# A weight fold spread over idle slots: its last part given slots of its own, and a buffer of its own

## The chip, the cores and the metric

The kernel runs on one core of one Trainium2 chip. The metric is the time of one execution on the device, in microseconds (us). Below, PE is the matmul engine (TensorE), PEld its weight loads, DVE the vector engine, ACT the scalar engine, POOL GpSimd and SP the engine whose queue issues most transfers.

## What is computed

One decoder layer on a batch of 16 sequences of 512 tokens and 256 features, all in float32: causal attention with 16 heads, LoRA terms on q and v and rotary positions, a residual and a layer norm, then a feed-forward part, a residual and a layer norm. The feed-forward part is the one that matters here:

```python
h = jnp.einsum('bsd,dh->bsh', x, W_exp) + b_exp
h = butterfly(h, up_weights, D_HIDDEN)
h = jax.nn.gelu(h + up_bias, approximate=False)
h = butterfly(h, down_weights, D_HIDDEN)
y = jnp.einsum('bsh,hd->bsd', h, W_con) + b_con
return y + down_bias
```

D_HIDDEN is 1024. A butterfly is ten linear stages; stage s mixes each pair of hidden units whose numbers differ in bit s. It is linear, so the kernel multiplies it into the weights once (the **fold**): the up side into W_exp, the down side into W_con. After that each sequence needs two plain matrix products, an expansion (256 to 1024) and a contraction (1024 to 256).

## The kernel before

**Slots.** All work is written out in one order by hand. The loop `for s in range(-head, last)` (line 827) runs over slots; five slots make one quad (half of the heads of one 128-feature chunk, even or odd), 20 slots one sequence b. In a slot, PE computes score blocks twice: `largest` (lines 411 to 442) for the row maxima, which DVE reduces (L430, "the reduces"), and `weights` (462 to 509), 15 slots behind, whose blocks ACT exponentiates (L493) and POOL masks (L497). The two kinds alternate in two PSUM tiles, pb and pa, with one buffer each: the pb and pa matmuls of a slot wait until exp and the reduces of the slot before have read them. Then come, in this order, `weigh` (probabilities times v, tile po, L521), the other tasks of the slot (`others[s]`), its `holes`, and last the fold tasks due in it (lines 870 to 876). Each engine runs its own instructions strictly in this order.

**Around slot 45.** For sequence 0, `turn_x1` stands in slot 45 (line 746): PE transposes the normed rows, DVE copies them to x1T (L617), POOL adds a bias over all of z (L621). `hidden` (628 to 646), the expansion product, takes slots 46 to 49, two of eight pieces a slot (tile ph, L633); DVE empties pieces 0 and 4 (L644), ACT the others (L646). Slot 50 has the gelus (ACT) and four projections of a later sequence (PE, tile pqk). `contract` (655 to 669), which reads the folded down weights `wdn`, starts in slot 51. `normalize` of sequence 0 (reciprocal and product on DVE, L553 and L554) is in slots 27, 28, 29, 31 and 36, 37, 39, 40.

**Fold tasks.** Every task is a pair (begin, rest). Begins run up to three tasks ahead of rests (line 872). There are these kinds:

- `across_chunks` (224 to 244): a stage 7, 8 or 9 for one pair of the eight 128-unit chunks. Begin is two ACT instructions into tiles x (tag `cross`, four buffers, L232), rest two DVE instructions (L239). The down side takes stages 9, 8, 7 in this order, four pairs each; the up side takes only stage 9 so.
- `across_by_products` (246 to 274): the same for stages 7 and 8 of the up side. Begin is four ACT instructions (L255), rest eight PE matmuls (L267, tile pd) and two ACT copies (L272).
- `multiply_paths` (205 to 215): six products on DVE (L215) that build, step by step, the matrices of stages 0 to 6 from path factors; the last is 1024 wide.
- `within_chunk` (217 to 222): such a matrix times one chunk; two PE instructions into a PSUM tile `fold` (L219) and an ACT copy (L222).
- `up_done` (291 to 298): four transposes (L294) and a DVE copy (L295) that put the folded up weights into `wup`.

`fold_tasks` (309 to 329) gives two lists. The first, the up side within chunks, is done in slots 3 to 14. The second has 44 tasks: 12 stage pairs, 6 products and 8 chunks of the down side, mixed evenly with 14 tasks of the up side, then four `up_done`. Lines 809 to 811 spread them evenly by count over slots 15 to 44.

**Buffers.** `yb` (line 113) is used twice: first for the path factors of the down side (loaded by `load_factors(1)`, line 127), then as `wup`. All PSUM tiles of the tag "w" (ph, fold, pd, pqk, pwo, py and the transposes) share three buffers.

## Time and profile before

| | us |
|---|---|
| median of three runs | 1359.33 |
| lowest, highest | 1358.64, 1360.84 |
| the profiled execution, its own time | 1357.15 |
| its span in the profile | 1355.4 |
| PE busy | 1320.3 |
| DVE busy | 925.8 |
| ACT busy | 707.3 |
| POOL busy | 510.9 |

The span is what the profile covers; 1.75 us of the execution lie around it. A row of the profile names the line, engine and operation, the tile written and those read, the number of instructions, their busy time and the mean of one in ns, and what ended the idle time ahead of them. A row of busy time by stretch has the stretch, its length, then PE, PEld, DVE, ACT and POOL busy with instruction counts, the clock granted to PE as a share of full speed, the busy share of the transfer engines and GB/s. A row of the timeline has a start, a duration and an instruction; equal neighbours are merged.

### The profile page before, as it was taken

How to read it: one execution, taken by the hardware profiler on the slowest of the kernel's cores; microseconds unless marked ns; L12 is line 12 of the kernel's file. 1: busy time of each engine (PE TensorE's matmuls, PEld its weight loads, DVE VectorE, ACT ScalarE, POOL GpSimd, SP SyncE). 2: the span in 40 equal slices, each digit the busy share in tenths (PEclk: the TensorE clock that was granted, in tenths of full speed). 3: DMA queues.
4: the chain of work that ended last, by engine and by line, in shares of the span. 5: the costliest groups of instructions: out<-in, count | busy, mean ns of one | idle time of the engine just before them, and what ended most of it. 6: DMA issues, size and time to landing. Idle time of an engine off the chain costs nothing.

```text
span 1355.4 us, 23859 instructions
## 1 busy us (share of the span) xinstructions
PE 1320.3 (97%) x8728; PEld 702.5 (52%) x8728; DVE 925.8 (68%) x2949; ACT 707.3 (52%) x1079; POOL 510.9 (38%) x777
## 2 busy tenths in 40 slices
PE   8898999999999999999999999999999999998998
PEld 4453545455454545555454554545555454554555
DVE  4788757667685766758577685857768685776632
ACT  2575454454646445464645545464554546445643
POOL 3534215344251533425153352515335252531311
PEclk9998999999999999999999999999999999999999
DMA  5311010110102011010110101010110101000000
GB/s 172 120 45 45 22 59 30 40 45 30 68 30 74 30 41 45 30 67 30 67 35 31 57 30 68 30 60 30 40 60 30 68 30 55 30 27 32 30 12 31
DMA packets 45685, 63.49 MB, mean 47 GB/s; under 512 B 5752, under 2 KB 26232, under 8 KB 45568
## 3 DMA queue, kind: packets, MB, share of 16 engines
q1 hardware_dynamic: 41680, 56.42, 11.8%
q10 hardware_dynamic: 3888, 5.55, 1.3%
q8 instruction: 69, 1.13, 0.3%
q14 instruction: 48, 0.39, 0.1%
HBM read 23.40 MB, written 8.91 MB: 24 GB/s over the span
## 4 chain that ended last, share of the span: by engine, by line
PE 84%; DVE 11%; ACT 3%; issue 2%; DMA 0%; POOLq 0%; POOL 0%; DVEq 0%; SPq 0%; ACTq 0%
PE pb L479 19%; PE ph L633 17%; PE py L660 16%; PE po L521 10%; PE pqk L337 8%; DVE junk L430 5%; PE pvv L383 4%; PE pwo L559 3%; PE pa L421 3%; DVE bn L577 1%; PE pb L421 1%; PE pt L616 1%; ACT pT L493 1%; PE pa L479 1%; DVE z L567 1%
## 5 line engine op out<-in xcount | busy, mean ns | idle before, releaser
L430 DVE CUSTOM_DVE_ANT_0 junk<-pa,causal 128x384 bf16<-128x384 f32 (+2 forms) x878 | 438.3, 499 | 235.0 <-PE pa L421 176.1
L493 ACT ACTIVATE pT<-pb 128x1024 f32<-128x1024 f32 (+1 forms) x314 | 293.8, 936 | 377.3 <-PE pa L421 227.6
L497 POOL TENSOR_SCALAR_AFFINE_SELECT pT<-pT 128x256 f32<-128x256 f32 x512 | 202.5, 407 | 733.3 <-ACT pT L493 731.6
L479 PE MATMUL pb<-qz,kz 17*128 17x512 f32 (+2 forms) x1756 | 328.8, 473 | 16.1 <-ACT pT L493 12.1
L421 PE MATMUL pa<-kz,qz 32*128 32x384 f32 (+3 forms) x1756 | 329.2, 474 | 4.2 <-DVE mx L430 4.2
L660 PE MATMUL py<-wdn,h 128*128 128x256 f32 x1024 | 252.1, 391 | 0.0
L479 PEld LDWEIGHTS pb<-qz,kz 17*128 17x128 f32 (+1 forms) x1756 | 142.9, 183 | 179.5 <-issue 82.2
L633 PE MATMUL ph<-x1T,yb 128*128 128x512 f32 x512 | 235.8, 604 | 0.0
L660 PEld LDWEIGHTS py<-wdn,h 128*128 128x128 f32 x1024 | 185.1, 189 | 72.2 <-issue 36.2
L521 PE MATMUL po<-pT,vaug 128*32 128x512 f32 (+3 forms) x2048 | 179.5, 446 | 0.0
L633 PEld LDWEIGHTS ph<-x1T,yb 128*128 128x128 f32 x512 | 92.4, 189 | 122.3 <-issue 97.6
L421 PEld LDWEIGHTS pa<-kz,qz 32*128 32x128 f32 (+1 forms) x1756 | 143.7, 184 | 13.6 <-DVE mx L430 11.2
L553 DVE RECIPROCAL sums<-sums 128x128 f32<-128x128 f32 x128 | 121.1, 946 | 0.0
L337 PE MATMUL pqk<-xT,wqk 128*128 128x512 f32 x256 | 118.5, 613 | 0.0
L646 ACT COPY h<-ph 128x512 f32<-128x512 f32 x84 | 49.2, 585 | 123.2 <-PE ph L633 123.2
L521 PEld LDWEIGHTS po<-pT,vaug 128*32 128x32 f32 x2048 | 47.1, 109 | 102.3 <-issue 78.2
L430 DVE DVE_READ_ACCUMULATOR2_ANT mx<- 128x1 f32 x1024 | 84.5, 82 | 0.0
L337 PEld LDWEIGHTS pqk<-xT,wqk 128*128 128x128 f32 x256 | 48.0, 194 | 61.9 <-issue 57.4
L365 POOL TENSOR_TENSOR swap<-swap,rope_sb 128x512 f32<-128x512 f32 x62 | 79.6, 1283 | 0.0
L602 ACT ACTIVATE z<-z,norm 128x256 f32<-128x256 f32 x128 | 66.7, 589 | 24.6 <-DVE norm L595 24.5
L668 DVE TENSOR_TENSOR z<-py,z 128x256 f32<-128x256 f32 x64 | 27.1, 423 | 74.1 <-PE py L660 73.9
L430 DVE CUSTOM_DVE_ANT_0 junk<-pb,causal 128x256 bf16<-128x256 f32 (+3 forms) x146 | 63.6, 436 | 17.3 <-PE pa L421 4.0
(91 smaller groups left out, 1334.2 us busy)
## 6 DMA issues: line engine op xcount, KB each, us to landing
xT<-in_xT SPq DMA_DIRECT2D x16, 512.0 KB
swap<-qz SPq DMA_DIRECT2D x64, 128.0 KB
swap<-kz SPq DMA_DIRECT2D x64, 128.0 KB
z<-in_x SPq DMA_DIRECT2D x16, 512.0 KB
sums<-x SPq DMA_DIRECT2D x64, 128.0 KB
out_y<-z SPq DMA_DIRECT2D x15, 512.0 KB
x<-x SPq DMA_DIRECT2D x32, 128.0 KB
early<-in_wexpT ACTq DMA_DIRECT2D x1, 1028.0 KB
```

Source lines behind the costliest of these rows:

```text
L337: nc.tensor.matmul(pq, wqk[:, d, e : e + P], xTs[b][:, d, :], start=(d == 0), stop=(d == NC - 1))
L365: engine.tensor_tensor(swap, swap, rope_sb[:, 1, :], ALU.mult)
L421: lambda i=i, rows=rows, at=at, n=n, t=t, ps=ps: nc.tensor.matmul(ps[:, i, at : at + n], q[rows, par, t * P : n], k_[rows, par, 0:n], star ...
L430: lambda i=i, at=at, n=n, t=t, g=g, ps=ps: nc.vector.tensor_tensor_reduce(out=junk[:, 0:n], in0=ps[:, i, at : at + n], in1=causal[:, T - n ...
L479: lambda i=i, rows=rows, at=at, n=n, k=block, ps=ps: nc.tensor.matmul(ps[:, i, at : at + n], kt[rows, par, k * P : (k + 1) * P], qt[rows, ...
L493: nc.scalar.activation(pT[:, heads, 0:n], ps[:, :, at : at + n], AF.Exp)
L497: nc.gpsimd.affine_select(out=diag, in_=diag, pattern=[[0, 2], [1, P]], compare_op=ALU.is_ge, fill=0.0, base=0, channel_multiplier=-1,)
L521: nc.tensor.matmul(po[HG * g : HG * (g + 1), k * P : T], vaugs[b % 2][:, k, NG * c + g, first : first + HG], pT[:, g, at : at + n], start= ...
L553: nc.vector.reciprocal(sums[:, ts], sums[:, ts])
L602: nc.scalar.activation(zs[b][:, t, :], zs[b][:, t, :], AF.Identity, bias=norm[:, 2, t : t + 1], scale=norm[:, 1, t : t + 1],)
L633: nc.tensor.matmul(ph, wup[:, c, hc * P : (hc + 1) * P], state["x1T", b][:, c, :], start=(c == 0), stop=(c == NC - 1),)
L660: nc.tensor.matmul(py, state["h", b][:, hc, t * P : (t + 1) * P], wdn[:, hc, :], start=(hc == 0), stop=(hc == NHC - 1),)
```

## The change

The down side's list is cut after its first eight tasks (stages 9 and 8). Those stay mixed with the up side; with `up_done` that is 26 tasks, spread by the same rule over slots 15 to 44. The other 18, in the old order (four pairs of stage 7, six products, eight chunks), form a third list, given by count to slots 45 to 49: four tasks, four, three, four, three. So the rests are the four pairs in slot 45, products 1 to 4 in slot 46, products 5 and 6 and the first chunk in slot 47, four chunks in 48, three in 49. The begins of the first two pairs run in slots 42 and 43. The path factors of the down side get a tile of their own (8128 bytes a partition), since `up_done` now writes `wup`, in `yb`, before they are used.

The tasks that stay are placed anew, too, since 26 and not 44 share the slots. Of the stages of the down side, stage 9 has its rests in slots 16, 19, 21 and 25 (before: 15 to 18), stage 8 in 28, 32, 34 and 38 (before: 19 to 22). Of the up side, the rests by products are in 15, 17, 18, 20, 23, 24, 26 and 27 (before: 15, 17, 19, 21, 23, 25, 27 and 29), those of stage 9 in 30, 31, 33 and 35 (before: 31, 33, 35 and 36), and `up_done` in 40 to 43 (before: 42, 42, 43, 44).

```diff
-    factors[1] = yb[:, 0:nfac]
+    factors[1] = const.tile([P, nfac], F32, name="factors1")
...
-        def down():
-            yield from all_across(1, wdn, D)
-            yield from all_within(1, wdn, D)
-
-
-        last = [
+
+
+        down = list(all_across(1, wdn, D))
+        late = down[2 * NHC // 2 :] + list(all_within(1, wdn, D))
+        up_last = [
             (idle, lambda d=d, half=half: up_done(d, half))
             for d in range(NC)
             for half in range(2)
         ]
-        return list(all_within(0, ya, DA)), mixed(down(), up()) + last
+        return list(all_within(0, ya, DA)), mixed(down[: 2 * NHC // 2], up()) + up_last, late
...
-    first, second = fold_tasks()
-    fold = first + second
+    first, second, third = fold_tasks()
+    fold = first + second + third
     tasks_at = dict(zip(range(2, behind), (0, 1, 2, 3, 4, 4, 5, 5, 5, 6, 9, 11, 14)))
-    for s in range(behind, 2 * per + 5):
-        tasks_at[s] = len(first) + -(-len(second) * (s - behind + 1) // (2 * per + 5 - behind))
+    needed = 2 * per + 5
+    for s in range(behind, needed):
+        tasks_at[s] = len(first) + -(-len(second) * (s - behind + 1) // (needed - behind))
+    for s in range(needed, needed + 5):
+        tasks_at[s] = len(first + second) + -(-len(third) * (s - needed + 1) // 5)
```

## The prediction

> **What bounds the kernel now.** I read the page first, then busy time by stretch, the waits of the matmul engine in the early stretch, and the order of instructions around slot 45.

> ```profile
> span 1355.4 us, 23859 instructions
> ...
> PE 1320.3 (97%) x8728; PEld 702.5 (52%) x8728; DVE 925.8 (68%) x2949; ACT 707.3 (52%) x1079; POOL 510.9 (38%) x777
> ...
> PE   8898999999999999999999999999999999998998
> ...
> DVE  4788757667685766758577685857768685776632
> ACT  2575454454646445464645545464554546445643
> ...
> PEclk9998999999999999999999999999999999999999
> ```

> PE (matmul) bounds nearly all of it; only the first five of 40 slices show idle PE and a lower clock. The whole fold lies there. By stretch (PE, PEld, DVE, ACT, POOL busy, clock):

> ```profile
> 55.43:93.39 37.96, 32.36 (x254) 17.85 (x254) 27.78 (x90) 32.46 (x77) 9.66 (x19) 1.00 0.08 27
> 93.39:121.98 28.59, 24.70 (x179) 11.70 (x178) 26.96 (x76) 15.88 (x31) 14.97 (x22) 1.00 0.18 63
> 121.98:166.21 44.23, 41.22 (x281) 22.12 (x282) 31.94 (x105) 21.50 (x38) 11.27 (x22) 0.85 0.07 23
> 166.21:189.75 23.54, 23.54 (x138) 10.19 (x137) 14.72 (x43) 8.70 (x12) 5.47 (x9) 1.00 0.10 34
> 189.75:198.45 8.70, 8.70 (x34) 3.42 (x33) 3.48 (x7) 8.03 (x12) 0.41 (x1) 1.00 0.20 75
> ```

> Slot starts come from the timeline of PE, where the pb and pa matmuls of each slot stand in order. These rows are slots 15-25 (**A**: ACT 86% busy), 26-33 (**B**: DVE 94%), 34-44 (**C**: PE at clock 0.85), 45-49 (**D**: PE without a gap, DVE 63%, ACT 37%), and 50. In A and B PE stands idle 66.55 - 57.06 = 9.5 us:

> ```profile
> PE pb L479 <- ACT pT L493: 5.7, 7, 1.9
> PE pa L421 <- DVE mx L430: 2.1, 3, 1.1
> ```

> The moved work, before:

> ```profile
> L239 DVE SCALAR_TENSOR_TENSOR wdn<-wdn,coefs,x 128x256 f32<-128x256 f32 x24 | 13.2, 591 | 0.0
> L219 PE MATMUL fold<-wdn,yb 128*128 128x256 f32 x16 | 6.1, 482 | 0.0
> L215 DVE TENSOR_TENSOR yb<-yb 128x32 f32<-128x32 f32 (+5 forms) x6 | 4.1, 690 | 0.1
> ```

> [...] L239 takes 0.478 at the median but 1.492 at most, as in the pair (two instructions, 1.90) that meets a POOL add:

> ```profile
> 130.76 1.90 DVE L239 SCALAR_TENSOR_TENSOR early<-early,coefs,x 128x257 f32<-128x257 f32 x2
> ```
> ```profile
> 130.87 1.49 POOL L367 TENSOR_TENSOR kz<-kz,swap 128x512 f32<-128x512 f32 x1
> ```

> [...] Here a window with 1.75 us of PE is followed by two at half:

> ```profile
> 118.40:121.80 3.40, 1.75 (x16) 0.91 (x16) 3.26 (x9) 1.02 (x1) 1.40 (x3) 0.99 0.04 11
> 121.80:125.20 3.40, 3.22 (x20) 1.61 (x24) 2.20 (x9) 0.76 (x2) 0.97 (x2) 0.50 0.00 0
> 125.20:128.60 3.40, 3.40 (x20) 1.89 (x16) 0.81 (x4) 2.58 (x6) 1.68 (x3) 0.51 0.00 0
> ```

> **The change, part by part.** All is set against the profiled execution (1357.15, of which 1355.4 span). The median of the runs is 1359.33, 2.18 above it; I add the difference to that median. No instruction is added or dropped: the lists are redistributed.

> *A, slots 15-25.* The list now holds 26 tasks for 30 slots, not 44, so tasks run thinner, and of the twelve stage tasks of the down side only four fall in A. By the lists, ACT loses eight pairs of L232 there (2 x 0.503 each, 8.0) and gets one more group of four L255 of the up side (1.3): -6.7 us of ACT; DVE loses seven or eight pairs of L239. What that buys is set slot by slot. Where ACT sent the exp late (slots 22 and 24-25) I take 0.4 and 0.7 us. In slots 16-19 exp and pair matmuls wait for each other anyway (pb must be read before the next pb): 0. In 20-21 a pd product moves one slot earlier and leaves the next without filler: +0.3. The rest, 0.2, is slot 23. **A: -1.0** (bounds -4 and +1).

> *B, slots 26-33.* DVE on the path loses 1.53 (the last stage-7 pair, seen in the trace), .18+.33+1.70+2.00 (six path products, two of them stretched by POOL) and the two L239 pairs of the up side (.88, 1.24): 7.9. It gets two stage-8 pairs and three pairs of the up side, about 5.9. That is 2.0 less. But two pd products of 2.0 us now fall in slots 26-27 (before 27 and 29), where PE has no gap, and starve DVE just ahead of the reciprocals of slots 27-31, which it then does late: +3.0. **B: +1.0** (bounds -2 and +2.5).

> *C, slots 34-44.* 16 fold matmuls go. The chain of waits has 10 of them on it, 2.01 + 0.44 + 0.43 + 0.70 = 3.6; the others lie behind exp or the reduces. In slot 34 the next wait, the reduces, allows some 1.4 of the 2.0; 37, 39 and 41 give 0.7, 0.45 and 0.6. A stage-8 pair in slot 38, where DVE decides, costs back 0.3. **C: -2.9** (bounds -5 and -1.5). up_done comes one to two slots earlier: nothing, DVE has it in either place.

> *D, slots 45-49.* (1) 16 matmuls of 128x256. Eight of that shape take 1.92 us in the contraction's chain, so 0.24 each: **+3.9**, wholly on the path, since PE has no gap here. (2) Slot 45 issues all four stage-7 pairs, eight L239. They queue on DVE after the two x1T copies, and ahead of the reduces of slot 46 that free pa for slot 47:

> ```profile
> 168.79 1.28 DVE L617 COPY x1T<-pt 128x512 f32<-128x512 f32 x2
> 169.03 2.36 POOL L621 TENSOR_TENSOR z<-z,bias 128x1024 f32<-128x1024 f32 x1
> 169.99 3.70 PE L633 MATMUL ph<-x1T,yb 128*128 128x512 f32 x8
> ```

> The copies end at 170.07, but POOL's bias add reads SBUF until 171.39, so the first L239 waits for it. Eight of 0.478 then end at 175.2. ACT gives no help: its tiles x have four buffers, and the third pair's begin (run before the first rest, tasks being begun three ahead) must wait for the first L239; four L232 then end at 173.9, and behind them waits exp of slot 46, which frees pb: 175.0. The reduces of slot 46 take 1.5, so pa is free at 176.8. PE is through with ph at 173.6; its pb pair fills about 0.3 of the gap: **+2.9** (from 1.6 without the POOL block to 4.5). (3) [...] one window of 3.4 at half clock is likelier than none: 3.4/2 = **+1.7** (0 to 3.4). (4) The six products (4.1 on DVE) lie under ph: two ph a slot are 3.63 us, and PE reaches the first fold of slot 47 just as the sixth product ends, 0 (up to 1.5 if POOL stretches them). The eight copies L222 (0.37) fit: ACT is 37% busy. Three PSUM banks turn over as fast as ACT copies (0.37 under 0.48 for a fold): 0. Slot 50 keeps its own bound, pqk 7.06 on PE over the gelus; the contraction of slot 51 reads wdn after the last copy, far behind. **D: +8.5** (bounds 5.5 and 11.7).

> *Own buffer.* The load at 40.3 goes elsewhere, same queue, same bytes; up_done no longer waits for the folds, which had ended before it anyway. 0.

> Sum: -1.0 + 1.0 - 2.9 + 8.5 = +5.6, giving 1362.8 for a profiled execution and **1364.9** for the median.

> **Rivals.** *Faster: the front is freed.* If ACT's late exp is what holds A and B, the thinner list recovers most of the 9.5 us idle on PE there. It decides from 5.6 us on (8.5 of D less 2.9 of C). For it: 5.7 us of waits for ACT pT. Against: most of those slots wait pb-exp-pb with ACT free before the exp, and B is short of DVE, not ACT. With 9.1 recovered: +8.5 - 2.9 - 9.1 = -3.5, 1355.8. *Same: D's stall is hidden.* DVE is 63% and ACT 37% busy in D; if the stage-7 pairs slip between the reduces without holding pa, D costs only the matmuls: -1.0 + 1.0 - 2.9 + 3.9 = +1.0, 1360.3. Against it: queues go in order, and all eight stand ahead of one slot's reduces. *Slower still:* a second window at half clock (1.7) and the first fold waiting for stretched products (1.5): 1368.1.

> **How the numbers follow.** Forecast 0.50, faster rival 0.13, same 0.20, slower still 0.17. A measurement of this kernel tells about 0.2% (2.7 us) from no change: faster 0.13, same 0.20, slower 0.67. The range leaves out the first rival alone, and reaches from the hidden stall with 2 us more from A and B (1358.0) to the slower rival and 1 us (1369.0).

> **What would show it.** In the profile after: a gap of PE before slot 47 that ends on DVE mx, some 3 us after the second ph; L232 of the third pair behind L239; a half-clock window in slots 47-48; no ACT or DVE wait in 48-49. A to C should be about 3 us shorter in all. I am wrong if the stretch from slot 15 to 45 shrinks by over 6 us, or if PE stays without a gap from slot 45 to 50.

## The result, and the profile after

The change made the kernel slower: 1373.22 us in the median of six runs (1368.42 to 1378.20) against 1358.99 (1355.32 to 1361.32); the ratio is 1.0109, with a 95% interval of 1.0081 to 1.0137. The forecast was 1364.9 in a range that ended at 1369.0: the sign was right, but it had +5.6 us where +14.2 came.

The page of the changed kernel (1371.81 us in its profiled execution). Its line numbers are one lower than before, from the function `fold_tasks` on.

```profile
span 1370.1 us, 23860 instructions
...
PE 1333.0 (97%) x8728; PEld 707.4 (52%) x8728; DVE 929.9 (68%) x2949; ACT 707.7 (52%) x1079; POOL 509.8 (37%) x777
...
PE   8898999999999999999999999999999999998998
...
DVE  5658766768576676857677585767758586775632
ACT  2465445464645546464554646455554645455543
...
PEclk9897799999999999999999999999999999999999
```

PE is busy 12.7 us longer with the same 8728 matmuls: they ran slower. The last line says why. Before, the granted clock fell below 9 in the fourth slice alone, to 8; now it is 8 in the second and 7 in the fourth and fifth, and its mean over the span is 0.981, not 0.993.

Busy time by stretch of the changed kernel (the columns are those of the prediction): slots 15-25, 26-32, 33-44, 45-49, and 50.

```profile
57.81:96.06 38.25, 34.16 (x254) 18.57 (x253) 20.32 (x74) 27.68 (x66) 7.55 (x17) 0.96 0.08 26
96.06:125.72 29.66, 25.97 (x158) 11.75 (x158) 23.85 (x64) 16.00 (x31) 12.82 (x17) 0.83 0.16 55
125.72:173.57 47.85, 42.78 (x285) 21.76 (x286) 38.17 (x120) 22.26 (x36) 15.39 (x27) 0.75 0.07 24
173.57:204.52 30.95, 29.73 (x153) 13.75 (x153) 20.98 (x56) 13.46 (x25) 5.51 (x9) 0.94 0.08 26
204.52:213.22 8.70, 8.70 (x33) 3.43 (x32) 3.47 (x7) 7.81 (x12) 0.41 (x1) 1.00 0.20 75
```

The same slots before, where the prediction cut at slot 34 and not 33:

```profile
93.39:116.33 22.94, 21.95 (x158) 10.40 (x157) 21.55 (x57) 14.12 (x29) 11.38 (x16) 1.00 0.18 65
116.33:166.21 49.88, 43.98 (x301) 23.41 (x302) 37.35 (x124) 23.26 (x41) 14.86 (x27) 0.86 0.08 26
```

So slots 15-25 changed by +0.3, 26-32 by +6.7, 33-44 by -2.0, 45-49 by +7.4, slot 50 by nothing. Another 2.4 us lie ahead of slot 15, where both kernels issue the same work (but for the order of two begins in slot 14). All of these but slot 50 have a lower clock than before: 0.96, 0.83 and 0.94 where it was 1.00, and 0.75 for 0.86 in slots 33-44.

Slots 45 to 49 went as the prediction drew them (timeline of the changed kernel):

```profile
177.38 4.43 DVE L239 SCALAR_TENSOR_TENSOR wdn<-wdn,coefs,x 128x256 f32<-128x256 f32 x8
179.14 1.71 ACT L232 ACTIVATE x<-wdn,coefs 128x256 f32<-128x256 f32 x4 [2.81 <-DVE wdn L239]
180.75 1.00 ACT L492 ACTIVATE pT<-pb 128x1024 f32<-128x1024 f32 x1
181.74 0.68 DVE L429 CUSTOM_DVE_ANT_0 junk<-pa,causal 128x512 bf16<-128x512 f32 x1
181.80 0.91 PE L478 MATMUL pb<-qz,kz 17*128 17x384 f32 x4 [0.72 <-ACT pT L492]
...
183.21 0.59 PE L420 MATMUL pa<-kz,qz 32*128 32x384 f32 x2 [0.50 <-DVE mx L429]
...
186.56 0.95 DVE L552 RECIPROCAL sums<-sums 128x128 f32<-128x128 f32 x1
...
187.75 1.95 DVE L215 TENSOR_TENSOR factors<-factors 128x512 f32<-128x512 f32 x2
...
190.40 0.59 PE L219 MATMUL fold<-wdn,factors 128*128 128x256 f32 x2
```

Eight L239 stand ahead of the reduces of slot 46 (L429); four L232 wait for them (2.81) and hold up exp (L492), which comes behind them on ACT; PE waits for both ahead of slot 47, 0.72 and 0.50 us. The first of the eight takes 1.66 us, beside POOL's bias add (L620, until 178.76), the other seven 0.47 each; so the wait that the prediction set there from one pair of before came. What the forecast had missed is the reciprocal at 186.56: `normalize` of the next sequence is due in slots 47 to 49, and it delays the last two products. Here, with PE at half clock from 183.90 to 187.31, ph keeps it busy until 190.56 and the products end at 189.70; in a trace without half clock there the first fold has to wait for them, 0.87 us (below).

In slots 28 to 30 the same trap stands, which the forecast did not look for:

```profile
110.13 0.87 DVE L239 SCALAR_TENSOR_TENSOR wdn<-wdn,coefs,x 128x256 f32<-128x256 f32 x2
110.70 0.91 ACT L232 ACTIVATE x<-early,coefs 128x257 f32<-128x257 f32 x2 [2.70 <-DVE wdn L239]
110.92 0.41 DVE L429 CUSTOM_DVE_ANT_0 junk<-pa,causal 128x256 bf16<-128x256 f32 x1
...
113.12 1.22 PE L478 MATMUL pb<-qz,kz 32*128 32x512 f32 x2 [2.67 <-ACT pT L492]
```

A begin (L232) waits 2.70 us for a rest (L239), since the new order begins three pairs, six tiles, for four buffers; PE then stands idle for 2.67, and the two matmuls that end the gap take 1.22, where two of the same shape take 0.70 at full clock (at 154.17 in the same trace).

### The profile page after: what moved, and what is told of

Same layout as the page of the kernel before. It is cut to its first block, busy times and chain, and to the rows that moved or that the text cites. A ratio compares the mean times of both kernels' runs of the same rounds, so it can differ in the third digit from the quotient of the medians.

```text
span 1370.1 us, 23860 instructions
## 1 busy us (share of the span) xinstructions
PE 1333.0 (97%) x8728; PEld 707.4 (52%) x8728; DVE 929.9 (68%) x2949; ACT 707.7 (52%) x1079; POOL 509.8 (37%) x777
## 2 busy tenths in 40 slices
PE   8898999999999999999999999999999999998998
## 3 DMA queue, kind: packets, MB, share of 16 engines
q8 instruction: 69, 1.13, 0.3%
## 4 chain that ended last, share of the span: by engine, by line
PE 86%; DVE 10%; ACT 2%; issue 2%; DMA 0%; POOLq 0%; POOL 0%; DVEq 0%; ACTq 0%
PE pb L478 19%; PE ph L632 17%; PE py L659 16%; PE po L520 11%; PE pqk L336 8%; DVE junk L429 4%; PE pvv L382 4%; PE pwo L558 3%; PE pa L420 3%; DVE bn L576 1%; PE pb L420 1%; PE pt L615 1%; PE pd L267 1%; ACT pT L492 1%; PE pa L478 1%
## 5 line engine op out<-in xcount | busy, mean ns | idle before, releaser
L429 DVE CUSTOM_DVE_ANT_0 junk<-pa,causal 128x384 bf16<-128x384 f32 (+2 forms) x878 | 438.1, 499 | 247.7 <-PE pa L420 186.5
L492 ACT ACTIVATE pT<-pb 128x1024 f32<-128x1024 f32 (+1 forms) x314 | 293.8, 936 | 375.0 <-PE pa L420 223.1
L478 PE MATMUL pb<-qz,kz 17*128 17x512 f32 (+2 forms) x1756 | 333.3, 478 | 19.6 <-ACT pT L492 16.9
L420 PE MATMUL pa<-kz,qz 32*128 32x384 f32 (+3 forms) x1756 | 334.5, 480 | 1.7 <-DVE mx L429 1.6
L520 PE MATMUL po<-pT,vaug 128*32 128x512 f32 (+3 forms) x2048 | 183.5, 454 | 0.0
L429 DVE DVE_READ_ACCUMULATOR2_ANT mx<- 128x1 f32 x1024 | 84.3, 82 | 0.0
L429 DVE CUSTOM_DVE_ANT_0 junk<-pb,causal 128x256 bf16<-128x256 f32 (+3 forms) x146 | 63.6, 436 | 18.9 <-PE pa L420 4.0
```

Source lines behind the costliest of these rows:

```text
L420: lambda i=i, rows=rows, at=at, n=n, t=t, ps=ps: nc.tensor.matmul(ps[:, i, at : at + n], q[rows, par, t * P : n], k_[rows, par, 0:n], star ...
L429: lambda i=i, at=at, n=n, t=t, g=g, ps=ps: nc.vector.tensor_tensor_reduce(out=junk[:, 0:n], in0=ps[:, i, at : at + n], in1=causal[:, T - n ...
L478: lambda i=i, rows=rows, at=at, n=n, k=block, ps=ps: nc.tensor.matmul(ps[:, i, at : at + n], kt[rows, par, k * P : (k + 1) * P], qt[rows, ...
L492: nc.scalar.activation(pT[:, heads, 0:n], ps[:, :, at : at + n], AF.Exp)
L520: nc.tensor.matmul(po[HG * g : HG * (g + 1), k * P : T], vaugs[b % 2][:, k, NG * c + g, first : first + HG], pT[:, g, at : at + n], start= ...
```

## The experiments

The first theory was that these waits for buffers make the loss of slots 26 to 32.

**Own buffer alone.**

```diff
-    factors[1] = yb[:, 0:nfac]
+    factors[1] = const.tile([P, nfac], F32, name="factors1")
```

> The kernel before with one line of the change: the path factors of the down side in a tile of their own. Theory (begins held up by the four buffers of the x tiles, which the new order of tasks causes) and rival (where the pd products and the DVE work now fall) both expect no change, 1359 within 3 us. If the buffer itself mattered (its address, its load), the time would go towards 1373.

Measured: 1358.95 (22 runs), ratio 1.0004 (0.9991 to 1.0018). The buffer costs nothing that 22 runs can tell. Its profiled execution has a span of 1363.8, though, 8.4 more than that of before with the same order: at a clock of 0.89 and not 0.94, slots 15 to 44 took it 115.6 us, not 111.3. From these two, an estimate: one trace of these slots is worth no more than some 5 us either way; the medians must decide there. Slots 45 to 49 vary far less: they take 23.53 or 23.54 in every trace that has nothing added there.

**Old places.** Empty tasks stand where those of the third list, the late part, were, so the tasks that stay keep the slots that they had before.

```diff
-        return list(all_within(0, ya, DA)), mixed(down[: 2 * NHC // 2], up()) + up_last, late
+        return list(all_within(0, ya, DA)), mixed(down[: 2 * NHC // 2] + [(idle, idle)] * len(late), up()) + up_last, late
```

> The changed kernel, but the tasks that stay in slots 15 to 44 keep the slots that they had before: empty tasks stand where the late ones were. Theory: the loss of 7 us in slots 26 to 33 is gone, because no begin there waits for a buffer; what is left is the loss in slots 45 to 50 (7.4 us in the trace) less what the emptier front gives (2 to 5 us), so 1361 to 1365. Rival (the late part alone makes the loss, by PE idling and its clock): 1371 or more.

**Six buffers for the x tiles.**

```diff
-    lora = const.tile([8, 4, D], F32, name="lora")
+    lora = ppool.tile([8, 4, D], F32, tag="pT", name="lora")
...
-                t = small.tile([P, cols], F32, tag="cross", name=f"x_{side}_{s}_{one}", bufs=4)
+                t = small.tile([P, cols], F32, tag="cross", name=f"x_{side}_{s}_{one}", bufs=6)
```

> The changed kernel with six buffers for the x tiles in place of four, so that three pairs can be begun ahead of a rest (room for them by moving the tile lora, read only at the start, into the ring of pT). Order and places as in the change. Theory: ACT no longer waits for DVE in slots 28 to 33 and 45; slots 26 to 33 get back about 5 us and slot 45 up to 1, so 1366 to 1368. Rival (placement, not buffers): 1372 to 1374.

**Both.**

> Both edits together: old places and six buffers. Theory: the only wait for a buffer left in the one with old places is that of slot 45, where DVE has eight instructions queued ahead of the reduces anyway, so no more than 1 us below the one with old places: 1360 to 1365. If the wait for the buffer is what makes the gap before slot 47, 3 us below it.

Measured: old places 1370.52, 1.0085 (1.0052 to 1.0117); six buffers 1372.09, 1.0102 (1.0080 to 1.0125); both 1369.86, 1.0078 (1.0051 to 1.0106). The theory falls. Six buffers do take the wait of ACT away, and the gap of PE stays (timeline of the kernel with six buffers):

```profile
108.04 0.90 ACT L232 ACTIVATE x<-early,coefs 128x257 f32<-128x257 f32 x2
...
110.28 1.01 DVE L239 SCALAR_TENSOR_TENSOR wdn<-wdn,coefs,x 128x256 f32<-128x256 f32 x2
...
113.25 1.22 PE L478 MATMUL pb<-qz,kz 32*128 32x512 f32 x2 [2.65 <-ACT pT L492]
```

L232 now runs at 108.04, ahead of L239, and PE still waits 2.65 us: DVE is late, as the prediction had it (two pd products in slots 26 and 27, none in 29). And with the old places, where no gap of PE in these slots is over 0.8 us, the loss is nearly all there. Slots 45 to 49 cost 7.4 to 7.8 us in all four kernels with a late part; the medians lie 10 to 14 above before. So the emptied front gains nothing and may lose. The new theory: PE's clock. A front with less for PE to do is granted half the clock for longer, which gives back what was taken out. In the three traces with the late part moved and old places or six buffers, and in the changed kernel, slots 34 to 40 have 17.1 or 20.5 us of half clock at a stretch; the kernel before and the one with only its own buffer, which have the chunk products there, have two shorter stretches each, of 6.8 and 3.4.

**Late part left out** (the contraction then uses unfinished weights), otherwise as old places.

```diff
-        return list(all_within(0, ya, DA)), mixed(down[: 2 * NHC // 2] + [(idle, idle)] * len(late), up()) + up_last, late
+        return list(all_within(0, ya, DA)), mixed(down[: 2 * NHC // 2] + [(idle, idle)] * len(late), up()) + up_last, []
```

> Old places, and the late part (stage 7, the six products and the eight chunk products of the down side) left out altogether; the contraction then uses unfinished weights. Theory (clock: a front with less work for PE is granted the lower clock for longer, so that what is taken out is given back): slots 45 to 50 last 23.5 us as before, the front is no shorter than before beyond 2 us, so 1357 to 1361. Rival (work: the front gets shorter by what was taken out, and the change lost it elsewhere): 1350 to 1356.

**Left out, but with its chunk matmuls in their old slots, read by nobody.**

```diff
+        def only_matmuls(c):
+            pb = bank(f"fill_{c}", [P, D])
+            nc.tensor.matmul(
+                pb, block(1, NSP - 1)[:, c * P : (c + 1) * P], wdn[:, c, :], start=True, stop=True
+            )
+
+        fill = [(idle, idle)] * 10 + [(idle, lambda c=c: only_matmuls(c)) for c in range(NHC)]
...
-        return list(all_within(0, ya, DA)), mixed(down[: 2 * NHC // 2] + [(idle, idle)] * len(late), up()) + up_last, []
+        return list(all_within(0, ya, DA)), mixed(down[: 2 * NHC // 2] + fill, up()) + up_last, []
```

> As the one that leaves the late part out, but the 16 chunk matmuls stand in their old slots 34 to 41, their results read by nobody. Clock theory: less of the half clock in slots 34 to 44 than without them, and a time not above it, 1354 to 1359, though PE has 3.9 us more to do. Rival (work): 2 to 4 us above the one without them.

**Late part late, and those matmuls besides** (the same edit, with `late` returned).

> Old places, the late part in slots 45 to 49 as in the change, and besides the 16 chunk matmuls once more in their old slots 34 to 41, read by nobody. Clock theory: the front is as before or better, only the 7.5 us of slots 45 to 50 are lost: 1364 to 1367, 3 us or more below the one with old places alone. Rival (work): 2 to 4 us above it, 1372 to 1375.

**Stage 7 early:** `late` is products and chunk products alone.

```diff
-        late = down[2 * NHC // 2 :] + list(all_within(1, wdn, D))
+        late = list(all_within(1, wdn, D))
...
-        return list(all_within(0, ya, DA)), mixed(down[: 2 * NHC // 2] + [(idle, idle)] * len(late), up()) + up_last, late
+        return list(all_within(0, ya, DA)), mixed(down + [(idle, idle)] * len(late), up()) + up_last, late
```

> Old places, and stage 7 stays in its old slots 23 to 26 as well; only the six products and the eight chunk products are late (three, three, three, three, two a slot from 45). If the gap of PE before slot 47 comes from the eight L239 of stage 7 in slot 45: no gap there, slots 45 to 50 last 23.5 + 3.9 = 27.4 us, at most 28.5 (products before the reduces), and the time is 3 to 4 us below the one with old places, 1366 to 1368. If it comes from the PSUM banks or the copies of the chunk products: 30 us or more, and no gain.

Measured: left out 1359.61, 1.0002 (0.9985 to 1.0019): 18 tasks fewer, no gain. With the matmuls back, 1358.30, 0.9983 (0.9967 to 1.0000): not slower, for 16 matmuls more; the difference of these two is within their intervals. Late part and matmuls: 1364.31, 1.0039 (1.0025 to 1.0053), 6 us below old places alone (1.0085, from 1.0052), with more work; the two intervals just touch. Stage 7 early: 1363.47, 1.0021 (1.0008 to 1.0035).

The traces show what the clock does. In those of the kernel before and of the changed one it stood, between two changes, for 3.41 us or a whole multiple of that (6.83, 10.24, 13.65, 17.07 and so on), so the rows below are 3.41 us long and cut where the clock changed. Without the chunk products (late part left out):

```profile
121.22:124.64 3.42, 2.57 (x18) 1.58 (x18) 2.99 (x10) 1.02 (x1) 2.00 (x3) 0.50 0.01 3
124.64:128.05 3.41, 3.19 (x28) 1.22 (x26) 2.15 (x10) 2.15 (x5) 1.30 (x3) 0.50 0.01 2
128.05:131.46 3.41, 3.38 (x20) 0.99 (x18) 1.58 (x5) 2.05 (x5) 1.34 (x3) 0.50 0.00 0
131.46:134.88 3.42, 2.78 (x12) 0.87 (x8) 3.01 (x7) 1.84 (x4) 1.75 (x2) 0.50 0.21 77
```

and with their matmuls back, with the first four of these (L325) as the timeline of PE has them:

```profile
123.12:126.54 3.42, 3.09 (x20) 1.80 (x24) 2.93 (x10) 0.28 (x1) 2.00 (x3) 0.50 0.01 2
126.54:129.95 3.41, 3.41 (x20) 1.69 (x20) 1.73 (x8) 2.61 (x5) 2.06 (x3) 0.50 0.00 0
129.95:133.36 3.41, 2.81 (x24) 1.07 (x24) 1.92 (x6) 1.96 (x4) 0.86 (x2) 1.00 0.00 0
133.36:136.77 3.41, 2.93 (x20) 1.10 (x16) 3.38 (x6) 1.32 (x2) 1.41 (x2) 1.00 0.21 77
```
```profile
128.33 1.91 PE L325 MATMUL fill<-wdn,factors 128*128 128x256 f32 x4
```

The third column from the end, the clock, is the point. Without the matmuls it is 0.50 in all four rows, and in none of them is PE busy throughout (2.57 to 3.38 us). With them, the four matmuls at 128.33 make the second row full (3.41 of 3.41 us), and the next is back at 1.00; 3.41 us more at half clock follow, from 136.77. (A full row was not always followed by 1.00: without the matmuls the 3.41 us from 134.88 are full, and the clock stays at half until 141.70.)

The loss of slots 45 to 49, from the first transpose of slot 45 to the projections of slot 50, stage 7 early (first) and late with the matmuls in the front (second):

```profile
169.69:196.84 27.15, 27.15 (x157) 13.05 (x153) 18.02 (x49) 12.01 (x22) 5.75 (x9) 1.00 0.09 30
```
```profile
170.10:200.56 30.46, 28.36 (x156) 13.23 (x152) 20.99 (x57) 13.54 (x26) 5.51 (x9) 1.00 0.08 27
```

Before it is 23.53. Products and chunk products cost 3.6 (PE without a gap, so the 16 matmuls), as expected, stage 7 another 3.3, and that with the clock at 1.00 throughout. The time of the kernel with stage 7 early is 3 us better than expected; the clock of its runs (0.985 in the mean, 0.983 with old places) would account for about that, by an estimate from these means (0.002 of 1364 us).

**Unread matmuls as a lever.** If the clock is the cause, matmuls in PE's idle time must help any kernel with this front.

```diff
+    def unread(s, cols, times=1):
+        ps = bank(f"unread_{s}", [P, cols])
+        for _ in range(times):
+            nc.tensor.matmul(ps, wqk[:, 0, 0:P], wqk[:, 0, 0:cols], start=True, stop=True)
...
             fold[given][1]()
             given += 1
+        if s in unread_at:
+            unread(s, *unread_at[s])
```

On the changed kernel, `unread_at = {29: (256, 4), 34: (256, 2)}` and `(256, 1)` in 36 to 41:

> The changed kernel, with matmuls added whose results nobody reads: four of 256 columns at the end of slot 29 (where the old order had a pd product and the new one leaves PE idle for 2.7 us), two in slot 34, one each in 36 to 41 (about where the chunk products were), 5.8 us of PE at full clock. Clock theory: the half clock between slots 29 and 40 (27 us in the trace) shrinks by more than half, the front is about as long as before, and only the loss of slots 45 to 50 is left: 1366 to 1369, 4 us or more below the change. Rival (work): 1375 to 1379.

On the kernel before, `(512, 1)` in 8, 12, 16, 18, 24, 32, 33 and `(256, 1)` in 20, 22, 30, 35, 38, 43:

> The kernel before, with unread matmuls at the end of thirteen slots after which PE stands idle in its trace (0.87 us each in slots 8, 12, 16, 18, 24, 32, 33, 0.48 each in 20, 22, 30, 35, 38, 43; 9 us of PE, against 12 us of gaps there). Clock theory: less half clock, and a time below the kernel before, 1350 to 1358. Rival (work): the same or up to 5 us longer.

On the changed kernel, `(512, 1)` in 8, 12, 16, 19, 21, 33, 38, 46, `(512, 2)` in 29, 32, `(256, 1)` in 25, 36, 43:

> The changed kernel, with unread matmuls at the end of the slots after which its own trace shows PE idle (0.87 us each in slots 8, 12, 16, 19, 21, 33, 38 and 46, two of them in 29 and 32, 0.48 each in 25, 36, 43). Clock theory: the half clock goes, and what is left against the kernel before with unread matmuls (1348.5) is slots 45 to 50 alone, less a front shorter by what was moved out of it (0 to 4 us): 1351 to 1357, some 17 us below the change. If the order of the front loses time by itself (DVE behind in slots 26 to 33), 1358 to 1361.

On the one with old places, those of the kernel before and `(256, 1)` in 36, 40, `(512, 1)` in 46:

> Late part in slots 45 to 49, the rest in its old places, with the unread matmuls of the kernel before with unread matmuls and three more (slots 36, 40, 46). Clock theory: the front shorter than 105 us by 0 to 4, slots 45 to 50 about 30.5: 1351 to 1356. If moving the late part out of the front is worth its 8 us of DVE and 7 us of ACT once the clock is held: under 1348.

Measured: the change with some of them 1369.87, 1.0062 (1.0045 to 1.0080); **the kernel before 1348.53, 0.9914 (0.9887 to 0.9942)**; the change with the clock held 1362.15, 1.0018 (1.0005 to 1.0032); old places with the clock held 1359.10, 0.9996 (0.9979 to 1.0014). The second is the version that beats both kernels: matmuls that nobody reads (13 groups, 0.59 to 1.13 us each in its trace; some 9 us of PE in all, as the author estimated) make it 12 us shorter, and its five runs lie within 1348.31 to 1349.78, where the 26 of the kernel before, beside it, spread from 1355.39 to 1369.03. The same rows of its page as above:

```profile
PE   8999999999999999999999999999999999999998
PEclk9999999999999999999999999999999999999999
```

The other three lie above what the clock theory expected, by 1, 5 and 3 us; the change with the clock held is nearest to the case in which the order of its front loses time by itself. In their traces a gap and some half clock are left around slot 33 (the change: 2.0 and 10.2 us; old places: 1.6 and 6.8), so the clock was not held everywhere. Even so, the change gained 11 us from unread matmuls.

**Off the path, or given back?** Left open was whether the DVE and ACT work that left the front was on the path. First, the late part left out (so the contraction uses unfinished weights again), its matmuls kept, with the unread matmuls of the kernel before; second, stage 7 early with the same.

> Late part left out (the contraction uses unfinished weights), its 16 chunk matmuls kept in their old slots and unread, and the unread matmuls of the kernel before with unread matmuls: against that kernel only 8 us of DVE and 7 us of ACT are missing in slots 15 to 44. If this work was on the path and its removal was given back through the clock: 1344 to 1346.5, slots 15 to 45 under 103.5 us. If it was off the path: 1348 to 1349, 105 us.

> Stage 7 in its old slots 23 to 26, products and chunk products from slot 45 on, the 16 chunk matmuls once more and unread in their old slots, and the unread matmuls of the kernel before with unread matmuls. Slots 45 to 50 cost 3.7 us more than before. If the products that left slots 27 to 32 (4.1 us of DVE) were on the path: 1347 to 1350. If not: 1351.5 to 1353.

Measured: 1348.92, 0.9924 (0.9912 to 0.9936), and 1354.28, 0.9957 (0.9941 to 0.9973). From the first pd product to slot 45, the kernel before with unread matmuls (first) and the one that leaves the late part out (second):

```profile
53.86:158.99 105.13, 100.71 (x745) 52.56 (x741) 87.66 (x271) 68.71 (x143) 35.91 (x61) 1.00 0.10 36
```
```profile
54.29:158.70 104.41, 100.50 (x746) 52.44 (x742) 79.64 (x257) 63.06 (x127) 35.10 (x61) 1.00 0.11 36
```

DVE has 8.0 us less to do, ACT 5.7, and the stretch is 0.7 shorter, the whole run no shorter. With PE this full, that work was off the path. The second lies 1.3 us above even the higher of its two cases, and its trace still has 13.6 us of half clock ahead of slot 45, so it decides nothing.

**The clock of every run.** The mean granted clock is on record for each run, not for the profiled ones alone. Over the 161 runs of the kernel before, all of them measured beside the experiments, it is 0.989 in the mean, for the six of the change 0.979. A run's length times what its clock lacks of 1 gives the full-clock time that PE was not granted: 15.4 us before, 28.8 in the change. It goes with the time within one kernel, too: in the change with some unread matmuls, the six runs at a clock of 0.992 to 0.995 took 1361.31 to 1366.81, the fifteen at 0.983 to 0.987 took 1369.06 to 1375.05. Among the runs of the kernel before, a straight line through the points gives 0.91 us of time for each us not granted. From these figures, an estimate: some 12 of the 14 us of the loss are the clock, and at an equal clock the change would cost about 2. Set at the clock of the kernel before in the same way, the late part left out (clock 0.985) would be 4 us shorter, just what its 16 matmuls take; with these matmuls back (0.990), less than 1, so the DVE and ACT work was nearly off the path without the unread matmuls too; late part and matmuls (0.990) would be 7 us longer, which is the loss of slots 45 to 49.

## Why the prediction was wrong

**Slots 45 to 49: right in mechanism, somewhat too large, and its parts off.** The forecast was +8.5; the traces show 7.4. The matmuls measured 3.6 for 3.9. The queue of eight L239 ahead of the reduces, with L232 and exp behind it, is there as drawn; stage 7 as a whole cost 3.3 where 2.9 for the gap and 1.7 for a half-clock window had been set, the latter as the author's estimate. In the late part with matmuls besides, the gap ahead of slot 47 is only 1.2 (0.74 and 0.49); 0.87 is a wait of the first fold for the products, which the reciprocals of the next sequence delay, and for 1.2 more PE is busy with the same matmuls (28.36 for 27.15). The half-clock window came (0.94 in the changed kernel), but at 1.00 the stretch takes 30.46 or, with old places, 31.23, for 30.93: with the half clock PE reached the first fold later (190.40) and no longer waited there. The two costs hid each other, so they must not be added. That the sum came so near is in part luck.

**Slots 15 to 44: this is the step that failed.** The prediction had A -1.0, B +1.0 and C -2.9, and in all three left the clock as the one trace of before had it. By the medians the front, that is all ahead of slot 45, lost about 7 us (14.2 less 7.4; with the ends of the interval, 4 to 11). In A, PE's idle time fell by 1.5 us (5.60 to 4.09), about as set, though ACT lost 4.8 us of work there and not 6.7; but a half-clock window made the same 254 matmuls 1.8 longer. Three terms of the working fell:

- "C: 16 fold matmuls go ... -2.9." They were on the chain of waits, and taking them out gained nothing: left out entirely, 1.0002, though some 4 us at an equal clock (the estimate above). The working priced a matmul by its time and left out the clock after it (without the 16 matmuls 20.5 us of half clock at a stretch, with them 6.8). The clock was priced for slots 47 and 48 only, and the windows at half clock in slots 34 to 44 were taken as given, although they lie just where PE loses work.
- "DVE on the path loses ... 7.9" in B. The chain put most of slots 26 to 33 on DVE, at 94% busy. With the clock held on both sides, 8.0 us of DVE less in the front is worth 0.7. So the chain over DVE showed who came last, not what its removal is worth.
- The gap by lateness of DVE in slots 28 and 29 was foreseen (+3.0) and measured 2.67; the half clock after it, 10.2 us long, was not. It makes most of the +6.7 of slots 26 to 32: PE is busy 4.0 us longer there with the same 158 matmuls.

**The range** took in a second half-clock window in slot 47, and the clock nowhere else. One profile of before made the front look firmer than it is: its clock, 0.993, is the highest that any of the 161 runs of this kernel reached, where their mean is 0.989, and the trace of the kernel with its own buffer, which issues the same work, has 0.986.

**The rivals.** "The front is freed" is refuted by the kernels that leave the late part out. "D's stall is hidden" is refuted by the gap and by the 3.3 us of stage 7. That the waits for buffers make the loss was my own first theory and fell with six buffers.

**What stays open.** How the loss of the changed kernel's front splits between the order of its tasks and the missing matmuls: with old places the ratio is 1.0085, with the new ones 1.0109, and their intervals overlap. So do the clocks of the six runs of each, 0.980 to 0.987 and 0.976 to 0.982. What exactly sets PE's clock was not shown: in the traces of before and of the change, 3.41 us at full clock with 2.12 to 2.93 us of PE are followed now by half, now by full clock.

## What to carry to other kernels

Where the clock of the matmul engine is below 1 in a stretch, work taken off that engine there is not a gain until a run shows it (here 18 tasks fewer gave 1.0002): price the clock of the stretches that follow, too, and look at the clock of many runs, not of one. Short matmuls whose results nobody reads, put where that engine would wait, can be worth more than the work that was moved: here some 9 us of them, by estimate, gave 12 us and took the spread out of the runs (1348.31 to 1349.78, before 1355.39 to 1369.03). And slots 45 to 49, where PE was full, had no room for what was moved into them: the matmuls were paid there in full (3.6 us), and the burst of vector work in one slot was paid by PE, which waited behind it (stage 7, 3.3 us).

## What the runs showed of the hardware that was not expected

The traces of the kernel before and of the changed one, from 30 to 250 us, cut into stretches of 3.41 us where the clock changed:

- Full clock turned into half ten times. In the stretch just ahead PE was busy for 1.65 to 2.93 us, and its longest gap there was 0.40 to 1.76 us, so in these ten cases PE never stood idle for a whole stretch.
- Half clock turned into full ten times, each time after a stretch in which PE was busy throughout. It went on into the next stretch nine times: PE was busy for 2.51 to 3.33 us in five of them, throughout in the other four (in the changed kernel from 43.95, 115.63, 129.28 and 139.52).

Short matmuls put into such a stretch can fill it, as the four at 128.33 did; the stretch after it was at full clock.
